# Negations on ScalarE, earlier first tiles, and a new order of a few steps at the joints of a two-layer graph kernel

## The chip, the cores and the metric

The kernel runs on one core of one Trainium2 chip, all in float32. The metric is device time in microseconds (us) of one whole execution. It is read as the median of several runs; a profile is one more execution, with its own time.

## The reference

x is 128 graphs of 64 nodes with 768 features; each graph has a 0/1 adjacency matrix of 64 x 64. After a first layer norm with ReLU, two graph layers follow, and the result is added to x. Cut to what matters:

```python
h = relu(layernorm(x))
for l in range(2):
    m_left  = h @ W_left[l].T ;  m_right = h @ W_right[l].T
    u_left  = h @ m_left^T / sqrt(768) ;  u_right = h @ m_right^T / sqrt(768)   # per graph, 64 x 64
    u = u_left * (upper triangle and diagonal of adj) + u_right * (transposed strict upper triangle)
    e = exp(u) * adj ;  attention = e / (sum(e) + 1e-10)
    h = relu(layer_norm(attention @ (h @ W_lin[l].T + b_lin[l])))
out = x + h
```

## The kernel before, in words

**Units.** The tokens are cut into 16 blocks of 512 (8 graphs each); a block is held transposed, features on the 128 partitions, in one of four tiles `ht0` to `ht3`. Two blocks make a superblock; a layer has eight. The first is called superblock 0 here and the next superblock 1.

**Pass one** of a layer (`pass_one`) computes the left and right products and the scores. A weight matrix is 3 x 3 pieces of 256 x 256, a superblock's tokens are 3 x 4 pieces; instead of 36 products of pieces, the table `PRODUCTS` (numbered 0 to 28) takes 29, of sums of weight pieces (`W_OPS`) with sums of token pieces (`X_OPS`), each once for the left side (k = 0) and once for the right side (k = 1). One such step is 8 matmuls and 8 weight loads on TensorE (PE), L530. The left side sums up in the PSUM banks X, Y and Z, the right side in V, `right0` and `right1`; `read` (L303 on ScalarE for a first value, L221 on VectorE for later ones) takes the banks into the tile `m`. After products 0 and 2 of a superblock the scores of the two blocks of the superblock before follow (`scores`, 192 small matmuls each, L472), and their softmax is a chain of small VectorE, ScalarE and SP steps (`chain`, L476 to L512).

**Superblock 0 of layer one** is special (`first`): it builds the weight sums itself, the left ones on VectorE, most right ones on GpSimd (`weight_op`, L180 to L186, where L186 is a negation: sums 16 and 27 have one each per side). Each finished sum is used by its product and stored to DRAM (`keep_weight`, L194); all later superblocks stream the sums back (`stream`, L197) into a ring of eight tiles `wp0` to `wp7`, each for a left and a right sum. While superblock 0 runs, ring tiles, `ht2`, `ht3` and others serve as single slots for weight sums: `Singles` hands them out by groups, each with the last product up to which a slot may be in use (20, 23, 25 or the end). Streams for products 0 to 4 of superblock 1 are put into SP's queue when product 25 is done (L698 to L700).

**Blocks 2 and 3** are prepared meanwhile: rows of x are loaded (L368), statistics taken on VectorE (L338, L339), scaled on ScalarE (L407, L412), transposed on VectorE (four steps L397 for each block), stored to DRAM in the transposed form (L394, four stores) and loaded back into `ht2` and `ht3` (`load_h`, L373). Blocks 0 and 1 are stored from `ht0` and `ht1` in superblock 1 (L727).

**Pass two** computes h W_lin the same way (15 products, `ORDER`, L1063), multiplies with the attention (L871, L894) and finishes the norm. Where layer two begins, its banks `right0` and `right1` lie where pass two of layer one had its `aux` banks, which are free when the last rows are scaled out of them (L1032, L1034).

**What sets the order.** Nothing is reordered by a scheduler: each engine runs its instructions in the order in which the Python code emits them. PE's steps set the beat: between the halves of a step and after it, `run(slot)` emits what was put into the dictionary `plan` for that slot, or else one item of the list `idle`. A superblock has 116 slots, four for each product. All loads and stores that matter here go through SP's queue, in order; in the built program each also waits until the transfer eight places ahead of it in that queue has landed, apart from its own data.

**Names for the steps of the prediction.** The wait for `SPq L394` is a store of a transposed block; `room<-in_x_dram` (L368) is a load of x rows, here the second half of block 3; `ht<-h` (L373) the load of a transposed block; `wp<-ws` (L197) a stream of a weight tile; `st` (L338) row statistics; `hl` the output of pass two's products; L492 to L506 the softmax (L494 is its exp on ScalarE). At the end of pass one the softmax of the last two blocks is emitted at L790 to L793: the first whole and two steps of the second at once, the rest into slots 3 to 15 of pass two.

Of the kernel before, what the change touches and what calls it, by code (L numbers as in the profile page):

```python
# [10 lines left out]
F32 = mybir.dt.float32  # L11
# [6 lines left out]
def kernel(  # L18
# [12 lines left out]
    nc = tc.nc  # L31
# [43 lines left out]
    def run(slot):  # L75
        if slot in plan:
            for f in plan.pop(slot):
                f()
        elif idle:
            f = idle.popleft()  # L80
            if f is not None:
                f()
# [97 lines left out]
    def weight_op(ss, kind, op, eng):  # L180
        i, o, sign, a, b = op
        t = ss.take((kind, o), LAST_W[o])
        if sign != "neg":
            added(eng, t, sign, ss[kind, a], ss[kind, b])
        else:
            eng.tensor_scalar_mul(t, ss[kind, a], -1.0)  # L186

# [32 lines left out]
    def added(eng, o, sign, a, b):  # L220
        (eng.tensor_add if sign == "+" else eng.tensor_sub)(o, a, b)  # L221
# [26 lines left out]
    def free(key):  # L248
        free_ts.append(held_ts.pop(key))
# [19 lines left out]
    def tokens(l, U, n):  # L269
        if n >= 12:  # L270
            return TS[l, U][n]
        j, k = divmod(n, 4)
        return HT[1, l, 2 * U + k // 2][:, j * K2:(j + 1) * K2, k % 2 * TH:(k % 2 + 1) * TH]
# [110 lines left out]
    def transpose_rows(l, u, pool=None):  # L384

        xr, todo = XR[l, u], []

        def turned(xr, pool):
            xb = blocks_tile(pool)

            def store():
                to = KEPT[l][u].rearrange("(b i) c t -> i c b t", b=4)
                for a in range(4):
                    nc.sync.dma_start(to[:, :, :, a * P:(a + 1) * P],  # L394
                                      xb[a * 32:(a + 1) * 32].rearrange("i (c b) q j -> i c b (q j)", b=4))

            return [lambda q=q: nc.vector.transpose(  # L397
                xb[:, :, q, :], xr[q].rearrange("p (b j) -> p b j", j=32)) for q in range(Q)], store

        if l == 0:  # L400
            mv = stat.tile([P, Q, 2], F32, name="mv0", bufs=2)
            sd = stat.tile([P, Q], F32, name="sd0", bufs=2)
            rs = stat.tile([P, Q], F32, name="rs0", bufs=2)
            nb = stat.tile([P, Q], F32, name="nb0", bufs=2)

            def scale():
                nc.scalar.activation(sd, mv[:, :, 1], AF.Sqrt, bias=eps_in)  # L407
                nc.vector.reciprocal(rs, sd)
                nc.vector.scalar_tensor_tensor(nb, mv[:, :, 0], -1.0, rs, op0=ALU.mult, op1=ALU.mult)

            def norm(q):
                nc.scalar.activation(xr[q], xr[q], AF.Relu, bias=nb[:, q:q + 1], scale=rs[:, q:q + 1])  # L412

            norms = [lambda q=q: norm(q) for q in range(Q)]
            stats = [lambda q=q: mean_var(mv[:, q, :], [xr[q][:, :HH], xr[q][:, HH:]]) for q in range(Q)]
            if u == 3:
                return stats, scale, norms, turned(xr, pool)
            for f in stats + none * (4 * (u < 4)) + [scale] + norms:
                todo.extend([f] + none * (u >= 4))
            todo.extend(none * (2 * (u < 4)))  # L420
        moved, store = turned(xr, pool)
        for f in moved:
            todo.append(f)
            todo.extend(none * (l or u >= 4))
        todo.append(store)
        return todo

# [6 lines left out]
    def pass_one(l, aside):  # L434
        with (tc.tile_pool(name=f"ps_one{l}", bufs=1, space=bass.MemoryType.PSUM) as ps,
# [81 lines left out]

            def project(U, weights, done):
                bank, seen, late = {}, (set(), set()), []
                for i, (w, t, at, new, what) in enumerate(PRODUCTS):  # L520
                    for k in range(2):
                        ns = S - 1 if k and U < NU - 1 else S
                        if new:
                            bank[k, at] = (right[at - 1] if k and at else
                                           ps_st.tile([P, 2 * TH], F32, name="V" if k else "XYZ"[at]))
                        p = bank[k, at][:, :NBB * ns].rearrange("p (g b s) -> p g b s", g=2, s=ns)
                        wk, tk = weights(i, k), tokens(l, U, t)
                        for g in range(2):
                            for c in range(K2):
                                nc.tensor.matmul(p[:, g], wk[:, c, g * P:(g + 1) * P],  # L530
                                                 tk[:, c, :].rearrange("p (b s) -> p b s", s=S)[:, :, :ns],
                                                 start=(new and g == c == 0), stop=(c == K2 - 1),
                                                 skip_group_check=True)
                            if g == 0:
                                run(4 * i + 2 * k)
                        late.append((k, p, ns, what))
                        if k and i in TURNS:
                            if U:
                                scores(2 * U - 2 + TURNS[i], both[TURNS[i]])
                            M[2 * U + TURNS[i]] = sp.tile([P, C, NBB, 2, S], F32, name="m", bufs=2)  # L540
                        now, late = late[::-1], []
                        for kk, pp, n, todo in now:
                            if any(2 * U + int(o, 16) % 4 // 2 not in M for o in todo[1::2]):
                                late.append((kk, pp, n, todo))
                                continue
                            read(pp, lambda o: M[2 * U + o % 4 // 2][:, o // 4 * K2:(o // 4 + 1) * K2,
                                                                     o % 2 * 4:o % 2 * 4 + 4, kk, :n], todo, seen[kk])
                        run(4 * i + 2 * k + 1)
                    for n, last in LAST_X.items():
                        if last == i and n >= 12:  # L550
                            free((l, U, n))
                    done(i)

            def streamed(U):
# [10 lines left out]
            def first():  # L565
# [7 lines left out]
                rest = [spared[:, 2 * n:2 * n + 2].rearrange("p c d -> p (c d)") for n in range(2)]  # L573
                rest.append(big.tile([P, K2, TH], F32, name="ts12", bufs=1).rearrange("p c t -> p (c t)"))
                put(SLOTS - 1, lambda: free_ts.append(12))
                ss = Singles(((20, chunks(2)), (23, chunks(3)), (25, early),
                              (NP, [s.rearrange("p (c d) -> p c d", c=K2) for s in rest]
                               + [room(n, 1).rearrange("p (c d) -> p c d", c=K2) for n in range(12, 15)]
                               + [s for n in range(5, RINGS) for s in pair(NP + n)])))
# [114 lines left out]
                def done(i):  # L694
                    for kind in "lr":
                        keep_weight(0, ss, kind, i)
                        dead(ss, kind, i)
                    if i == 25:  # L698
                        for n in range(5):
                            stream(0, NP + n)  # L700

                return (lambda i, k: ss["lr"[k], PRODUCTS[i][0]]), done

# [16 lines left out]
            for U in range(NU):  # L720
# [3 lines left out]
                    put_token_ops(l, U, "after")  # L724
                if l == 0 and U == 1:
                    for n in range(2):
                        put(20 + 6 * n, lambda n=n: nc.sync.dma_start(KEPT[0][n], HT[1, 0, n]))  # L727
                if U + 1 < NU:
                    def block(n, slot):
                        u = 2 * U + 2 + n  # L730
                        if (l, u) == (0, 3):
                            stats, scale, norms, (moved, store) = transpose_rows(l, u)
                            for fs, at in ((stats[:2], (57, 60)), (stats[2:], (66, 68)), ([scale], (72,)),
                                           (norms, (74, 75, 76, 77)), (moved, (79, 81, 82, 83))):
                                for f, s in zip(fs, at):
                                    put(s, f)
                            put(87, store)
                            put(SLOTS - 4, lambda: load_rows(l, 4))
                            put(101, lambda: load_h(1, l, u))
                            return  # L740
                        *todo, store = transpose_rows(l, u)
                        slot = put_all(slot, todo)
                        put(slot + 6, store)
                        if u + 1 < NB:
                            put(slot + 7, lambda: load_rows(l, u + 1, halves=(1,) if (l, u) == (0, 2) else (0, 1)))
                        slot = max(slot + 15, 92) if U == 0 and l == 0 else slot + 15
                        put(slot, lambda: load_h(1, l, u))
                        if l:
                            put_all(slot + 20, affine(1, l, u))
# [40 lines left out]
            one, two = softmax(NB - 2), softmax(NB - 1)  # L790
            for f in one[:4] + two[:2] + one[4:]:
                f()
            put_all(3, two[2:])  # L793

    rows = {}

# [406 lines left out]
```

## Time and profile before

| | us |
|---|---|
| median of 3 runs | 2714.45 (2713.27 to 2717.49) |
| the profiled execution | 2710.28 |
| its span in the trace | 2708.5 |
| PE busy (matmuls) | 2677.3, 99% of the span |
| VectorE (DVE) busy | 1502.9, 55% |
| GpSimd (POOL) busy | 1380.6, 51% |
| ScalarE (ACT) busy | 829.2, 31% |

The profiled execution took 1.8 us more than its span, and 4.2 us less than the median of the runs; changes in the trace are counted against 2710.28 and then carried over to the median. The span is 99% PE, so the reading is one of gaps: the trace lists, for each group of instructions, the idle time of its engine ahead of it in brackets with what ended it. DVE, ACT and POOL are busy for half the time or less on average; an average over 2.7 ms doesn't tell whether they are full in a stretch of 15 us. A line of the timeline reads: start, duration, engine, line, operation, output<-inputs, sizes, count, and the bracket. SPq is the SP queue issuing a transfer, DMA a transfer on its way. PE's matmul ends are modelled by the profiler, so gaps of a few tenths are rough.

### The profile page before, as it was taken

The numbers are of one execution on the slowest core, as the hardware profiler recorded it, in microseconds if no ns is written. First come the engines' busy times: TensorE is split into PE (matmuls) and PEld (weight loads), VectorE is DVE, ScalarE is ACT, GpSimd is POOL, SyncE is SP. The second block draws the span as 40 slices with busy tenths as digits, with TensorE's granted clock in tenths as the row PEclk, the third lists the DMA queues.
The fourth block names the chain that finished last, engine by engine and source line by source line (L and its number), as shares of the span: only waits on it lengthen the run. The fifth ranks groups of instructions, "written<-read, shape, count | busy, mean of one in ns | idle before, by whom it ended". The sixth has DMA issues, their size and how long they took to land.

```text
span 2708.5 us, 47300 instructions
## 1 busy us (share of the span) xinstructions
PE 2677.3 (99%) x18514; PEld 2304.5 (85%) x18514; DVE 1502.9 (55%) x2458; ACT 829.2 (31%) x1615; POOL 1380.6 (51%) x1071
## 2 busy tenths in 40 slices
PE   9899999999999999999999999999999999999998
PEld 7788888888888888888788888888888888888886
DVE  7665655756647433334343645546446475666667
ACT  4032131321310254454631221221212304445443
POOL 5633244333336776566433325334244286887886
PEclk9999999999999999999999999999999999999999
DMA  8886966858765345558585956958759524655655
GB/s 268 273 304 208 286 204 205 280 203 263 243 209 179 98 144 180 169 168 259 180 279 176 308 190 220 283 185 287 227 194 302 211 79 133 185 157 159 185 156 148
DMA packets 310223, 567.81 MB, mean 210 GB/s; under 512 B 62833, under 2 KB 190065, under 8 KB 301809
## 3 DMA queue, kind: packets, MB, share of 16 engines
q1 hardware_dynamic: 309840, 564.39, 65.1%
q8 instruction: 148, 2.42, 0.4%
q14 instruction: 75, 0.61, 0.1%
q10 hardware_dynamic: 160, 0.39, 0.0%
HBM read 429.40 MB, written 135.27 MB: 208 GB/s over the span
## 4 chain that ended last, share of the span: by engine, by line
PE 94%; DVE 2%; DMA 1%; SPq 1%; issue 0%; ACT 0%; DVEq 0%
PE right L530 17%; PE X L1063 12%; PE X L530 11%; PE V L530 10%; PE Z L530 9%; PE Y L530 9%; PE V L1063 8%; PE Y L1063 6%; PE both L472 5%; PE Z L1063 4%; PE aux L871 2%; PE aux L894 1%; PE Y L894 0%; DMA wp<-ws 0%; PE Z L472 0%
## 5 line engine op out<-in xcount | busy, mean ns | idle before, releaser
L221 POOL TENSOR_TENSOR ts<-ht 128x512 f32<-128x512 f32 x352 | 479.7, 1369 | 160.7 <-PE X L1063 65.9
L221 POOL TENSOR_TENSOR ts<-ht,ts 128x512 f32<-128x512 f32 x192 | 253.0, 1325 | 348.5 <-PE V L530 208.2
L530 PE MATMUL right<-ts,wp 128*128 128x252 f32 (+1 forms) x1632 | 381.1, 377 | 1.5 <-DVE wp L221 1.5
L530 PEld LDWEIGHTS right<-ts,wp 128*128 128x128 f32 x1632 | 310.5, 190 | 40.0 <-DVE wp L221 1.9
L481 POOL TENSOR_TENSOR wm<-adj,tri 128x256 f32<-128x256 f32 x60 | 42.2, 726 | 493.9 <-DMA wp<-ws 220.7
L221 DVE TENSOR_TENSOR m<-m,X 128x512 f32<-128x512 f32 x160 | 105.6, 685 | 259.6 <-ACT m L303 181.3
L221 DVE TENSOR_TENSOR m<-m,right 128x504 f32<-128x504 f32 (+1 forms) x304 | 199.5, 673 | 87.5 <-PE right L530 73.5
L1063 PE MATMUL X<-room,ts 128*128 128x256 f32 x1024 | 244.1, 380 | 0.2
L221 POOL TENSOR_TENSOR ts<-ht,ht 128x512 f32<-128x512 f32 x128 | 163.5, 1288 | 140.0 <-PE right L530 93.7
L530 PE MATMUL Z<-ts,wp 128*128 128x256 f32 x992 | 234.5, 380 | 0.1
L1063 PEld LDWEIGHTS X<-room,ts 128*128 128x128 f32 x1024 | 192.0, 190 | 31.3 <-issue 1.8
L530 PEld LDWEIGHTS Z<-ts,wp 128*128 128x128 f32 x992 | 188.8, 190 | 24.8 <-issue 0.4
L530 PE MATMUL X<-ts,wp 128*128 128x256 f32 x872 | 207.5, 381 | 0.0
L530 PE MATMUL V<-ts,wp 128*128 128x252 f32 (+1 forms) x864 | 201.7, 377 | 0.0
L303 ACT ACTIVATE m<-right 128x504 f32<-128x504 f32 (+1 forms) x64 | 36.1, 590 | 510.2 <-PE both L472 490.3
L380 ACT ACTIVATE ht<-ht,b_col,a_col 128x512 f32<-128x512 f32 x192 | 140.8, 803 | 144.0 <-DMA ht<-h 144.0
L530 PEld LDWEIGHTS X<-ts,wp 128*128 128x128 f32 x872 | 164.9, 190 | 22.8
L1063 PE MATMUL Y<-room,ts 128*128 128x256 f32 x768 | 182.6, 380 | 0.0
L530 PEld LDWEIGHTS V<-ts,wp 128*128 128x128 f32 x864 | 164.4, 190 | 20.2
L1063 PEld LDWEIGHTS Y<-room,ts 128*128 128x128 f32 x768 | 146.1, 190 | 20.1 <-issue 0.6
L221 DVE TENSOR_TENSOR m<-m,Y 128x512 f32<-128x512 f32 x144 | 95.8, 683 | 115.1 <-PE Y L530 104.6
L1029 POOL TENSOR_TENSOR z<-z,b 128x768 f32<-128x768 f32 x62 | 112.6, 1830 | 89.8 <-DVE z L1026 89.8
(225 smaller groups left out, 4845.0 us busy)
## 6 DMA issues: line engine op xcount, KB each, us to landing
wp<-ws SPq DMA_DIRECT2D x435, 512.0 KB, 6.4
ht<-h SPq DMA_DIRECT2D x62, 1536.0 KB, 8.7
h<-room SPq DMA_DIRECT2D x112, 384.0 KB, 6.9
z<-z SPq DMA_DIRECT2D x128, 192.0 KB, 3.1
ws<-wp SPq DMA_DIRECT2D x93, 256.0 KB, 4.4
xr<-in_x_dram SPq DMA_DIRECT2D x120, 192.0 KB, 3.6
out_dram<-xr SPq DMA_DIRECT2D x120, 192.0 KB, 2.6
room<-z SPq DMA_DIRECT2D x112, 192.0 KB, 5.2
```

What stands on the lines that cost most here:

```text
L221: (eng.tensor_add if sign == "+" else eng.tensor_sub)(o, a, b)
L303: nc.scalar.activation(to(o), p, AF.Copy, scale=1.0 if sign == "+" else -1.0)
L380: nc.scalar.activation(ht, ht, AF.Relu, bias=cols[1][:, c:c + 1], scale=cols[0][:, c:c + 1])
L472: nc.tensor.matmul(p[h * S + e:h * S + e + 32, q, e:e + 95], ht[:, c, b * S + e:b * S + e + 32], mb[:, e:e + 95], start=(c == 0), stop=(c ...
L481: nc.gpsimd.tensor_tensor(wm[:, :, k], adj[:, :, 1 - k], tri[:, k].unsqueeze(1).to_broadcast([P, Q, S]), op=ALU.mult)
L530: nc.tensor.matmul(p[:, g], wk[:, c, g * P:(g + 1) * P], tk[:, c, :].rearrange("p (b s) -> p b s", s=S)[:, :, :ns], start=(new and g == c ...
L871: nc.tensor.matmul(cx[k][i, m, :HH], at[j, q, :], hl[j, q, m * HH:(m + 1) * HH], start=True, stop=True)
L894: nc.tensor.matmul(parts[r, k][n][i], at[j, q, :], hl[j, q, cut], start=True, stop=True)
L1029: nc.gpsimd.tensor_add(zs[k], zs[k], rows["b"])
L1063: nc.tensor.matmul(p[:, n], b[t][:, c, r * P:(r + 1) * P], w[s][:, c, :], start=(i in FIRST and i not in PRELOAD and n == c == 0), stop=(c ...
```

## The change

Six edits:

1. A negation of a weight sum that stood on VectorE is done on ScalarE (two instructions, left sums 16 and 27 of superblock 0). Those on GpSimd stay.
2. The four transposing steps of block 2 get an empty slot after each, as those of later blocks have. Its store and the load after it move four slots with them.
3. In superblock 0, the load of transposed block 2 moves from slot 92 to 85, that of block 3 from 101 to 98, the load of the rows of block 4 from slot 112 to 105; the streams of the weight tiles of products 0 and 1 of superblock 1 are put in after product 23 and not 25, for which four single slots are limited to product 23.
4. The stores of blocks 0 and 1 in superblock 1 move from slots 20 and 26 to 26 and 34.
5. In superblock 0 of layer two, the order of the steps is product 0 left, product 1 left, product 0 right, product 1 right and so on; before, product 0 right came second.
6. The last steps of the second softmax at the end of pass one: in place of slots 3, 4, 5, ... they take 6, 9, 12, 13, 14, ...

```diff
-            eng.tensor_scalar_mul(t, ss[kind, a], -1.0)
+        elif eng is nc.vector:
+            nc.scalar.mul(t, ss[kind, a], -1.0)
+        else:
+            eng.tensor_scalar_mul(t, ss[kind, a], -1.0)
...
-            todo.extend(none * (l or u >= 4))
+            todo.extend(none)
...
+                steps = [(i, k) for i in range(NP) for k in range(2)]
+                if l and not U:
+                    steps[1], steps[2] = steps[2], steps[1]
+                for n, (i, k) in enumerate(steps):
...
-                ss = Singles(((20, chunks(2)), (23, chunks(3)), (25, early),
+                ss = Singles(((20, chunks(2)), (23, chunks(3) + early[:4]), (25, early[4:]),
...
-                    if i == 25:
-                        for n in range(5):
-                            stream(0, NP + n)
+                    for n in {23: (0, 1), 25: (2, 3, 4)}.get(i, ()):
+                        stream(0, NP + n)
...
-                        put(20 + 6 * n, lambda n=n: nc.sync.dma_start(KEPT[0][n], HT[1, 0, n]))
+                        put(26 + 8 * n, lambda n=n: nc.sync.dma_start(KEPT[0][n], HT[1, 0, n]))
...
-                            put(SLOTS - 4, lambda: load_rows(l, 4))
-                            put(101, lambda: load_h(1, l, u))
+                            put(SLOTS - 11, lambda: load_rows(l, 4))
+                            put(98, lambda: load_h(1, l, u))
...
-                        slot = max(slot + 15, 92) if U == 0 and l == 0 else slot + 15
+                        slot = max(slot + 15, 85) if U == 0 and l == 0 else slot + 15
...
-            put_all(3, two[2:])
+            put_all(put_all(6, two[2:4], 3), two[4:])
```

The rest of the diff rewrites the loop of `project` over the list `steps`; outside superblock 0 of layer two it emits the same steps in the same order.

## The prediction

> **What bounds the kernel now.** I read the page's first part, then PE's idle times one by one, then SP's and VectorE's timeline ahead of the large ones.
>
> ```profile
> span 2708.5 us, 47300 instructions
> PE 2677.3 (99%) x18514; PEld 2304.5 (85%) x18514; DVE 1502.9 (55%) x2458; ACT 829.2 (31%) x1615; POOL 1380.6 (51%) x1071
> ```
>
> PE is the bound: 31.2 us of the span are not PE, and the change leaves PE's instructions as they are, so 31 us is a ceiling. The timeline of PE gives its stalls (start, duration, ..., in brackets the idle time before and its releaser). The eight that concern the edits:
>
> ```profile
> 57.13 1.97 PE L530 MATMUL Y<-ts,room 128*128 128x256 f32 x8 [0.67 <-DVE room L221]
> 60.55 1.97 PE L530 MATMUL right<-ts,wp 128*128 128x252 f32 x8 [1.46 <-DVE wp L221]
> 88.64 1.97 PE L530 MATMUL Y<-ts,ht 128*128 128x256 f32 x8 [1.82 <-DVE ht L186]
> 122.30 1.97 PE L530 MATMUL Y<-ht,wp 128*128 128x256 f32 x8 [2.58 <-DMA wp<-ws]
> 132.09 1.02 PE L472 MATMUL both<-m,ht 128*32 128x95 f32 x38 [2.75 <-issue]
> ...
> 901.73 1.97 PE L1063 MATMUL X<-room,ht 128*128 128x256 f32 x8 [1.39 <-ACT hl L303]
> ...
> 1363.12 1.94 PE L530 MATMUL right<-ht,wp 128*128 128x252 f32 x8 [1.34 <-DVE z L1032]
> ...
> 2235.92 1.97 PE L1063 MATMUL X<-room,ht 128*128 128x256 f32 x8 [0.67 <-ACT hl L303]
> ```
>
> They sum to 12.7 us. The first five lie in superblock 0 of layer one and the start of superblock 1, the others at three joints. Between them PE is full, so a gain before a stall is kept only if what ends that stall also comes earlier. For that I read SP's timeline:
>
> ```profile
> 61.45 4.66 SPq L394 DMA_DIRECT2D h<-room  x4
> 66.15 1.91 SPq L194 DMA_DIRECT2D ws<-room  x1
> 68.11 1.74 SPq L194 DMA_DIRECT2D ws<-wp  x1
> 69.95 2.26 SPq L368 DMA_DIRECT2D room<-in_x_dram  x4
> ...
> 104.56 0.47 SPq L373 DMA_DIRECT2D ht<-h  x1
> ...
> 112.93 8.73 SPq L197 DMA_DIRECT2D wp<-ws  x5
> ```
>
> and two rows of VectorE's:
>
> ```profile
> 61.30 2.82 DVE L221 TENSOR_TENSOR wp<-ht 128x512 f32<-128x512 f32 x2
> ...
> 87.19 1.30 DVE L186 TENSOR_SCALAR ht<-wp 128x512 f32<-128x512 f32 x1
> ```
>
> The chain of waits follows from the second-half load of block 3 (landed 76.92) through row statistics at 77.15 and a VectorE that is full until the negation ends at 88.49. It also shows the stream at 112.93 released by the block load of 104.56, landing at 112.87: that load stands eight places ahead of it in SP's queue, and SP waits for such a landing.
>
> [...] The nearest row, 128x512 from SBUF to SBUF with bias and scale columns (L380), took 803 ns; I use 0.8[...]. [...] the two sums at 61.30 took 1.41 us each beside a busy GpSimd, a like one at 59.84 0.65. [...] The page's instruction queue q8 shows 148 packets, 2.42 MB, 16.4 KB each; one falls at 98.5 us and the next at 129.5.
>
> **Part by part** (negative is time saved; against the profiled 2710.28).
>
> *Second softmax later (edit 6).* At 901.73 PE waits for the read of bank X by ScalarE, which stands behind the exp at 900.68, and that behind VectorE's sum at 900.23. In the changed order that exp stands behind two more reads. Product 2 ends on PE at 898.45, so the read can be done by 899.25 and PE goes on at 900.34: −1.39; at 2235.92 likewise −0.67. New cover: the rest of VectorE's chain, 4.2 us of steps, now runs from 904.6 to 908.8, and the reads that come next can't start before 909.15 (bank X of product 8): 0.35 us of air at worst. The eight small stores of that softmax stand 7 slots later in SP's queue; their reader is the last block of pass two, hundreds of us later. In layer one six loads of raw weights pass them; nobody waits for those on PE. Sum −2.06.
>
> *Order of two steps (edit 5).* PE's `right` at 1363.12 waits until 1362.98 for the last scaling out of the old banks. Product 1 left (bank Z, free, its weights streamed and its tokens scaled) takes 1.73 us there: `right` could start at 1363.3, after the release: −1.34. `right` ends no later than now, so ScalarE's reads behind it keep their times.
>
> *Negations on ScalarE (edit 1).* The first (36.47 on VectorE, 0.64) gains nothing: the read of Z two instructions later waits for PE's end at 37.46 and started at 37.70. On ScalarE it holds up two copies by some 1.7 us that are used at 46. The second frees VectorE of 1.30 us and shortens PE's wait: 0.8 on ScalarE, 0.5 less. Queued behind it on ScalarE are the four scalings of block 3 (from 85.36); the transposes that need them follow in time.
>
> *Transposes of block 2 spaced (edit 2).* The weight that releases 60.55 loses one transpose (0.89) ahead of it: PE goes on at 59.65. But the next weight sum but two (64.65 to 65.73) stays behind all four transposes, and PE needs it at once: of 0.9 some 0.2 is left at 66.10. What gets later: the last transpose ends at 64.1, not 61.3, so the stores L394 start 2.75 later, and so, past the same two weight stores, does the second-half load of block 3. It lands at 76.92 + 2.75 = 79.7. VectorE stands at its statistics from 77.05: 2.6 us idle. Work from there to the sum that is negated took 77.15 to 87.09; now to 89.7. Plus 0.8: product 20 starts on PE at 90.55 against 88.64, **+1.9**. This contains all gains before it, also 66.10. I take the landing as certain to 0.7 us either way.
>
> *First tiles and block loads sooner (edit 3).* From product 20 to the end of product 28 PE took 88.64 to 119.72, 31.08; so PE reaches superblock 1 at 121.63. Block 2's load is now released by the store of sum 20 (about 94.3) in a stretch where the DMA share was under 0.4, not at 104.56; stream 0 needs the landing of sum 23's store, put at 108 to 110, with no 1.5 MB load right ahead of it, and should land by 115 (9.23 us after its issue, as now, would still be 119). The wait of 2.58 goes, and PE starts at 121.63 instead of 122.30. Net of edits 1 to 3: **−0.67**. Block 3's load lands near 118.5 (now 119.7).
>
> *Then the gap of 2.75 in the scores.* Nothing on the core releases it; a 16 KB instruction packet moves at 129 to 130, PE goes on at 132.09, and the DMA share is 1.01 to 1.07 there. The 31 other scores of the trace have no gap over 0.7. After: 1.57 MB (block 2) has left the full stretch, about 4 us at 400 GB/s, and the eight row loads can start at about 118.6 and not 124.2. The queue is shorter when PE asks, but perhaps not empty. Bounds 0 (or a few tenths worse) and −2.75; I take −2.1, as the queue is nearly through.
>
> *Stores of blocks 0 and 1 (edit 4).* They move 5 to 7 us later; their tiles are reloaded at slot 49, about 12 us after the later start of the first. Streams run eight products, 27 us, ahead. Nothing; without that cover a late stream costs what it lacks.
>
> Sum: −2.06 −1.34 −0.67 −2.1 = −6.2: 2704.1 for a profiled run. The median is 4.2 above the profiled one, so 2708.3.
>
> **Rivals.** (B) *The fetch gap stays.* For it: all bytes but one load are still to be moved before 135. Sum −4.1: 2710.4, and with a half gain 2709.0. (C) *The second-half load isn't late in effect* (DMA is idle from 52 to 62, so two weight stores leave early and the queue is emptier), or VectorE catches up on a quieter GpSimd: product 20 at 88.0 or so, another −1.9 to −2.6: 2705.7 to 2706.4; with the fetch gap as in B, 2707.8. Against it: same four stores, same two stores behind. (D) *Slower: the row load of block 3 is so late that VectorE's wait outweighs all joints.* Product 20 starts 10.85 us after the landing; the total is worse than before when the delay of product 20 is over 2.58 (the wait that it eats) + 3.4 (the joints), a start after 94.6, so from a landing at 83.8, 4.1 later than I put it. At 86 it gives 2714.45 + 8.2 − 2.6 − 3.4 = 2716.7, without any fetch gain. Against it: the chain had 5.15 us from issue to landing under an already full DMA.
>
> **How the numbers follow.** A measurement of this kernel can tell about 0.2%, 5.4 us, from no change: the line is 2709.0. A 0.42 (2707.6 to 2709.0), B 0.33 (2709.0 to 2712), C 0.18 (2704.5 to 2708), D 0.07 (2714.5 to 2718). Faster by over 0.2%: A most of it, C, a little of B: 0.57. Within: 0.39. Slower: D's far end, 0.04. A and C and B up to 2712.5 make the range 2704.5 to 2712.5; it leaves out D and a tail.
>
> **What would show it.** Right: no ScalarE wait at the first X after the joints; `right` at layer two without a wait; statistics of block 3's second half waiting near 79.7 and product 20 waiting longer than 1.82; no wait for wp<-ws at superblock 1. Wrong: a wait on a stream or a block load there, new waits of PE for hl reads after the joints, or a product 20 that starts by 88.6 (then C). The gap in the scores decides A against B.

## The result and the profile after

The changed kernel takes 2706.89 us (median of 14 runs, 2704.2 to 2710.12), the kernel before 2713.13 us in the runs beside them: a ratio of 0.9976, 95% interval 0.9968 to 0.9984. The profiled execution takes 2705.84 us, 4.4 less than that of before. The medians moved by 6.2 (by the interval 4.3 to 8.7).

```profile
span 2704.1 us, 47306 instructions
PE 2677.7 (99%) x18514; PEld 2301.3 (85%) x18514; DVE 1499.1 (55%) x2456; ACT 832.4 (31%) x1617; POOL 1381.4 (51%) x1071
```

PE is busy about as long as before (2677.7 against 2677.3), so what went is idle time. PE's timeline at the places of the prediction:

```profile
59.45 1.97 PE L535 MATMUL right<-ts,wp 128*128 128x252 f32 x8 [0.59 <-DVE wp L223]
80.64 1.94 PE L535 MATMUL right<-ts,ht 128*128 128x252 f32 x8 [0.24 <-DVE m L223]
84.51 1.97 PE L535 MATMUL X<-ts,wp 128*128 128x256 f32 x8 [1.93 <-DVE wp L223]
89.61 1.96 PE L535 MATMUL Y<-ts,ht 128*128 128x256 f32 x8 [1.43 <-ACT ht L186]
120.52 1.89 PE L535 MATMUL Y<-ht,wp 128*128 128x256 f32 x8
130.19 1.02 PE L474 MATMUL both<-m,ht 128*32 128x95 f32 x39 [2.78 <-issue]
...
899.35 1.89 PE L1069 MATMUL X<-room,ht 128*128 128x256 f32 x8
...
1360.90 3.56 PE L535 MATMUL right<-ht,wp 128*128 128x252 f32 x16
...
2231.57 1.89 PE L1069 MATMUL X<-room,ht 128*128 128x256 f32 x8
```

A line without a bracket is work ahead of which the view lists no idle time: the three joints (1.39, 1.34 and 0.67 before) and the start of superblock 1 (2.58 before, now 120.52 instead of 122.30). Three things stay or are new: product 19 left waits 1.93 at 84.51, product 20 starts 0.97 later than before (89.61), and the gap in the scores is 2.78, where it was 2.75.

SP's and VectorE's timelines show why product 20 is later:

```profile
62.60 4.66 SPq L396 DMA_DIRECT2D h<-room  x4
67.30 3.80 SPq L196 DMA_DIRECT2D ws<-wp  x2
71.20 1.94 SPq L370 DMA_DIRECT2D room<-in_x_dram  x4
```

```profile
78.10 1.02 DVE L340 BATCH_NORM_STATS2 st<-room 128x6 f32<-128x384 f32 x2 [2.10 <-DMA room<-in_x_dram]
...
82.74 1.63 DVE L223 TENSOR_TENSOR wp<-ht 128x512 f32<-128x512 f32 x1
```

```profile
88.83 0.63 ACT L186 ACTIVATE ht<-wp 128x512 f32<-128x512 f32 x1 [6.82 <-DVE wp L223]
```

The stores of block 2 start at 62.60 (61.45 before), the load behind them at 71.20 (69.95), and the statistics wait 2.10 for it. From there VectorE is full until the negation on ScalarE, which takes 0.63 us.

Summed at the trace: superblock 1 starts 1.78 earlier, the joints give 3.40, together 5.2; PE's busy time is 0.4 longer and small gaps of a few tenths elsewhere take back about as much. This execution was also 0.3 late from its start (a product that begins at 54.59 in the profile of before begins at 54.89 here), ahead of what the edits change; so of the 0.97 by which product 20 is later, 0.3 are not theirs.

### The profile page after: what moved, and what is told of

Read it like the earlier page. It is cut to its first block, busy times and chain, and to the rows that moved or that the text cites. A ratio compares the mean times of both kernels' runs of the same rounds, so it can differ in the third digit from the quotient of the medians.

```text
span 2704.1 us, 47306 instructions
## 1 busy us (share of the span) xinstructions
PE 2677.7 (99%) x18514; PEld 2301.3 (85%) x18514; DVE 1499.1 (55%) x2456; ACT 832.4 (31%) x1617; POOL 1381.4 (51%) x1071
## 4 chain that ended last, share of the span: by engine, by line
PE 96%; DVE 1%; SPq 0%; issue 0%; DMA 0%; ACT 0%; DVEq 0%; ACTq 0%
PE right L535 17%; PE X L1069 12%; PE X L535 11%; PE V L535 11%; PE Z L535 9%; PE Y L535 9%; PE V L1069 8%; PE Y L1069 6%; PE both L474 5%; PE Z L1069 4%; PE aux L877 2%; PE aux L900 1%; PE Y L900 0%; PE Z L474 0%; DVE wp L223 0%
## 5 line engine op out<-in xcount | busy, mean ns | idle before, releaser
L223 DVE TENSOR_TENSOR hl<-hl,V 128x512 f32<-128x512 f32 (+1 forms) x136 | 89.2, 656 | 128.9 <-PE V L1069 118.7
```

## The experiments

Each ratio is taken against the kernel before in the same session (2712.2 to 2714.0 in the four sessions, which ran on three chips). Where a run is compared with the changed kernel, the difference is that of the two medians, across sessions; through the two ratios it is smaller (2.2 and not 3.4 in experiment 4, 2.4 and not 3.1 in experiment 7). The intervals of experiments 3 to 9, where there is one, all overlap that of the changed kernel, experiment 8's only just. So what a single edit moves is read from the traces. Intervals are of 95%. Undoing an edit means the lines marked with a minus in the diff of the change are put back.

**1. The joints alone** (edits 5 and 6 on the kernel before).

```diff
+                if l and not U:
+                    steps[1], steps[2] = steps[2], steps[1]
...
-            put_all(3, two[2:])
+            put_all(put_all(6, two[2:4], 3), two[4:])
```

> The kernel before with edits 5 and 6 alone (order of two steps at layer two, later steps of the second softmax). Theory: the three waits of 1.39, 1.34 and 0.67 us go and nothing takes their place; superblock 0 of layer one is as before (product 20 waits 1.8, superblock 1 waits 2.6 for its tile): 3.4 us less, about 2709.7 against 2713.1. Rival: PE runs ahead into instruction fetches or reads that come no sooner and gives part back: 1 to 2 us less.

Measured: 2710.16 us, ratio 0.9987 [0.998, 0.9993], 3.5 less (1.9 to 5.4 by the interval). In the trace the three joints have no wait; superblock 0 is as before (product 20 at 88.42 after 1.84, the stream waits 2.92). The prediction's 3.4 for these two edits stands.

**2. Superblock 0 alone** (edits 1 to 4, the joints undone).

```diff
-                if l and not U:
-                    steps[1], steps[2] = steps[2], steps[1]
...
-            put_all(put_all(6, two[2:4], 3), two[4:])
+            put_all(3, two[2:])
```

> The changed kernel with edits 5 and 6 undone: edits 1 to 4 alone. Theory: superblock 1 starts 1.6 us sooner as in the trace of the changed kernel, the gap in the scores stays near 2.8: about 2711.5 against 2713.1. Rival: runs without the profiler often have a smaller gap in the scores, since the median of the changed kernel fell by 6.2 and its traced span by 4.4: then 2.5 to 3.5 us less.

Measured: 2711.11 us, ratio 0.9989 [0.9983, 0.9996], 2.5 less. Product 20 starts at 90.20 after 1.43, superblock 1 at 121.11 without a wait; in the scores there are two gaps, 1.36 and 1.93. With the joints' 3.5 that makes 6.0 of the 6.2: the two halves add up within their intervals. The means differ by 3.1, and the mean granted clock of the runs (0.9982 here, 0.9976 in the runs of before beside them) accounts for 1.8 of it: these runs lost less time at a lower clock, of which experiments 7 to 11 tell more.

**3. Block 2's transposes close together again** (edit 2 undone in the changed kernel).

```diff
-            todo.extend(none)
+            todo.extend(none * (l or u >= 4))
```

> The changed kernel with edit 2 undone (transposes of block 2 close together). Theory: the late second-half load of block 3 is what holds product 20: the load lands near 76 instead of 78.0, product 20 starts at 88.0 to 88.4 instead of 89.6, superblock 1 at about 119.3 instead of 120.7; product 12's right step waits 1.4 again, which is lost in it: 1.4 us less than the changed kernel, 2705.5. Rival: VectorE's work and not its wait sets product 20; it stays at 89.6 or gets later, no gain or 0.5 us more.

Measured: 2705.62 us, ratio 0.9974 [0.9965, 0.9983], 1.3 less than the changed kernel by the medians, with overlapping intervals. Its trace is 2.05 us late from the start for a reason of its own (a wait of 2.08 at 11.56 and a stretch at a clock of 0.50 behind it, 12.09 to 15.50; the product that begins at 54.89 in the changed kernel begins at 56.94). With 2.05 subtracted, product 20 starts at 88.60 (89.61) and superblock 1 at 119.51 (120.52), 1.0 earlier, where 1.2 to 1.6 was expected for product 20. Only 0.3 of it lies ahead of the statistics (77.79 against 78.10, now without a wait); 0.7 lies behind them, where one VectorE sum took 1.18 instead of 1.63, of which the last section tells more. So the trace points to a small cost of edit 2, and neither it nor the medians settle its size.

**4. The load ahead of the stores** (changed kernel; the load of block 3's second half stands before the four stores of block 2 in SP's queue).

```diff
+                        if (l, u) == (0, 2):
+                            put(slot + 6, lambda: load_rows(l, 3, halves=(1,)))
                         put(slot + 6, store)
-                        if u + 1 < NB:
+                        if u + 1 < NB and (l, u) != (0, 2):
```

> The changed kernel with the second-half load of block 3 put ahead of the four stores of block 2 in SP's queue. Theory: it lands near 68, the row statistics wait for nothing, product 19 waits less than 0.3, product 20 starts at 87.4 or sooner, superblock 1 at about 118.5: 2.2 us less than the changed kernel, 2704.7. Rival: VectorE is full of work there, the wait of 2.1 only moves; product 20 gains under 0.5, or the later store delays block 2's load and superblock 1 waits for it.

Measured: 2703.48 us, ratio 0.9968 [0.9955, 0.998], 3.4 less than the changed kernel.

```profile
62.60 1.74 SPq L370 DMA_DIRECT2D room<-in_x_dram  x4
64.39 5.11 SPq L396 DMA_DIRECT2D h<-room  x4
```

```profile
86.72 1.97 PE L535 MATMUL Y<-ts,ht 128*128 128x256 f32 x8 [1.19 <-ACT ht L186]
126.98 1.02 PE L474 MATMUL both<-m,ht 128*32 128x95 f32 x39 [2.46 <-issue]
```

The load leaves SP at 62.60 instead of 71.20, VectorE's statistics start at 75.91 without a wait for it, and product 19's wait is gone. Product 20 starts at 86.72, 2.89 sooner, superblock 1 at 117.63, 2.89 sooner as well. So the late load was the cause of the later product 20. Of the 2.89, 2.19 are the earlier statistics (75.91 against 78.10); the other 0.70 come behind them, mostly from the VectorE sum of 1.63 that took 1.18 here.

**5. The instruction stream shifted** (changed kernel with 64 more PE instructions, 32 tiny matmuls and their weight loads, ahead of product 20). If the gap belongs to a place in PE's instruction stream, it goes or moves; if it belongs to the time, it stays.

```diff
+                    if (l, U, i, k) == (0, 0, 20, 0):
+                        for _ in range(32):
+                            nc.tensor.matmul(both[1][:32, :32], KEEP["ident"][:, :32], KEEP["ident"][:, :32],
+                                             start=True, stop=True)
```

> The changed kernel with 32 tiny matmuls of 32 rows by 32 columns (64 PE instructions with their weight loads) on the unused bank both1 ahead of product 20, in the time in which PE waits there; their result is thrown away. Theory: [...] the gap of 2.8 falls under 0.5, 2.3 us or more less than the changed kernel. Rival: the gap is due to full DMA queues at that time[...], or to the scores' own data: it stays at 1.5 to 3.

Measured: 2705.77 us, ratio 0.9973 [0.9962, 0.9984], 1.1 less than the changed kernel. The first scores, which were cut in two after 153 matmuls, are whole:

```profile
125.81 4.13 PE L474 MATMUL both<-m,ht 128*32 128x95 f32 x192
...
140.49 1.68 PE L474 MATMUL both<-m,ht 128*32 128x95 f32 x72 [0.92 <-issue]
```

The gap of 2.78 is gone, though the transfers on the queues are the same; 0.92 comes back in the second scores, and some tenths elsewhere; every later instruction stands 64 places further on in the stream too. The tiny matmuls take 2.21 us, of which 1.4 lie in the wait that product 20 had anyway. Hence less than expected in time, but the place of the gap follows the instruction. The time at which the scores start is no rival: in experiment 9 the same scores start at 125.75, 0.06 earlier than here, and have a gap of 2.52.

The packet records of the traces show what stands beside these gaps. In the nine kernels that don't shift the stream, a 16 KB packet of the instruction queue q8 begins between 1.2 us before and 0.9 us after PE stops in the first scores, and PE goes on 1.4 to 1.7 us after that packet has ended (in the changed kernel: PE stops at 127.41, the packet runs from 127.56 to 128.58, PE goes on at 130.19). The smaller gaps in the second scores, 0.12 to 1.93 in seven traces, end in the same way, 1.3 to 1.4 after a packet. Here, with the stream shifted, the last packet ahead of the first scores runs at 114.56, eleven us before they start.

**6. Fewer bytes** (changed kernel without six of the eight row loads of block 4, so that block is computed from other rows). If the gap does not depend on the bytes in the queues, it stays.

```diff
-            for a in range(4):
+            for a in range(1 if (l, u) == (0, 4) else 4):
```

> The changed kernel with six of the eight row loads of block 4 left out (1.2 MB less in the stretch ahead of the scores; block 4 is then computed from other rows). Theory of full queues: the fetch comes through sooner, the gap falls under 1.2. [...] the gap stays over 2.

Measured: 2706.82 us in a single run.

```profile
130.16 1.22 PE L474 MATMUL both<-m,ht 128*32 128x95 f32 x39 [3.56 <-issue]
```

Taking 1.2 MB off the queues left the gap, at 3.56, and the packet ahead of its end began later than in any other trace, 0.87 us after PE had stopped. The DMA share at 126 to 132 was still 0.93 to 1.07, so this run does not exclude that empty queues would shorten it; it does show that this much relief doesn't.

**7. Tiles and loads as late as before** (edit 3 undone in the changed kernel).

```diff
...
-                    for n in {23: (0, 1), 25: (2, 3, 4)}.get(i, ()):
-                        stream(0, NP + n)
+                    if i == 25:
+                        for n in range(5):
+                            stream(0, NP + n)
...
-                        slot = max(slot + 15, 85) if U == 0 and l == 0 else slot + 15
+                        slot = max(slot + 15, 92) if U == 0 and l == 0 else slot + 15
```

> The changed kernel with edit 3 undone (loads and first tiles at their old places). Theory: superblock 1 waits for its first tile again, and since the store of block 3 is some 0.5 us later than before, PE starts it at 122.4 to 122.9 instead of 120.7: 1.7 to 2.2 us more than the changed kernel, about 2708.8. Rival: the stalls at products 19 and 20 are what set the start; it stays within 0.5.

Measured: 2710.04 us, ratio 0.9985 [0.9979, 0.9992], 3.1 more than the changed kernel. PE:

```profile
122.60 3.31 PE L535 MATMUL Y<-ht,wp 128*128 128x256 f32 x8 [1.98 <-DMA wp<-ws]
...
134.43 1.81 PE L474 MATMUL both<-m,ht 128*32 128x95 f32 x39 [3.17 <-issue]
```

The wait for the stream is back with 1.98, and superblock 1 starts at 122.60, as expected. But the product behind it took 3.31 us instead of 1.89, and the scores behind the gap 1.81 instead of 1.02. The view by stretches says why (columns: stretch and length, then the busy time of PE, PEld, DVE, ACT and POOL with instruction counts, the granted clock of TensorE, DMA share, GB/s):

```profile
119.70:123.10 3.40, 1.42 (x7) 0.97 (x6) 1.81 (x3) 0.00 (x0) 3.08 (x3) 0.99 1.04 410
123.10:126.50 3.40, 3.40 (x9) 2.70 (x8) 0.00 (x0) 0.00 (x0) 3.32 (x4) 0.50 0.94 290
126.50:129.90 3.40, 3.40 (x107) 2.97 (x109) 0.00 (x0) 0.00 (x0) 3.32 (x3) 1.00 1.00 387
```

After a stretch in which PE was idle for 1.98 us the clock was 0.50 for 3.4 us, and 1.7 us of work were lost on top of the wait. Such stretches come in some executions and not in others: eight of the 21 runs had a mean clock of 0.999 and took 2707.0 us on average, the seven with 0.997 took 2711.3. So part of the 3.1 beyond the expected 1.7 to 2.2 is theirs; how much, the medians don't tell.

**8. Both steps together** (experiments 4 and 5 in one kernel).

> The changed kernel with both: the second-half load of block 3 ahead of the stores of block 2, and the 64 PE instructions ahead of product 20. If the two theories hold and add: 3.0 + 2.3 less than the changed kernel, about 2701.6. If the gap stays, as the kernel with the load first alone, 2703.5.

Measured: 2701.04 us, ratio 0.9956 [0.9944, 0.9969], the fastest kernel here: 5.9 less than the changed one and 12 less than before. It was forecast at 2701.6. Products 19 and 20 do not wait at all, and both scores run whole (`x192`).

**9. The negation back on VectorE** (edit 1 undone in the changed kernel).

```diff
-        elif eng is nc.vector:
-            nc.scalar.mul(t, ss[kind, a], -1.0)
```

> The changed kernel with the four negations of superblock 0 back on VectorE (edit 1 undone), all else kept. Theory: one negation took 0.63 us on ScalarE in the changed kernel and 1.4 us or so beside VectorE's full stretch before; of block 3's chain to product 20 one negation lies on the path, so product 20 starts 0.6 to 1.0 us later (about 90.4 instead of 89.61) and superblock 1 at about 121.4 instead of 120.68, with the gap in the scores of 2.3 to 3.2 us as it is: 2707.5 to 2708 (+0.7 to +1.0). Rival, in which the negations don't lie on the path since the load of block 3's rows sets the end: superblock 1 at 120.7, 2706.9 (no change from the changed kernel).

Measured: 2707.66 us, ratio 0.9978 [0.997, 0.9986]: 0.8 more than the changed kernel, too little for the intervals to tell. Product 20 did not start near 90.4, as expected, but at 89.63. Still the trace shows the edit: product 20 started 11.13 us after the statistics of block 3's second half (78.50 to 89.63), where experiments 6 and 7, with the negation on ScalarE, took 10.43 and 10.45: 0.7 for the edit. (The superblock start that this expectation calls 120.68 reads 120.52 in the trace, and edit 1 moves two negations, not four.) In the changed kernel and experiment 2 the same way took 11.5 and 11.6, since one sum of VectorE (82.74) took 1.63 and 1.77 instead of 0.68. That difference of 1.0 is not this edit's: it goes with how the sum meets one of GpSimd (last section).

```profile
83.96 1.97 PE L533 MATMUL X<-ts,wp 128*128 128x256 f32 x8 [0.98 <-DVE wp L221]
89.63 3.65 PE L533 MATMUL Y<-ts,ht 128*128 128x256 f32 x8 [2.00 <-DVE ht L186]
```

Here too the product behind the wait of 2.00 took 3.65. Such a slow product follows some waits of about 2 us and more and not others (the product behind the 2.58 of before took 1.97). The next two runs ask when.

**10 and 11. Stalls of a chosen length** (experiment 8's kernel with 14 stalls in layer one; N is 1, then 4).

```diff
+                    if U and l == 0 and (i, k) in ((20, 0), (26, 0)):
+                        nc.tensor.matmul(both[1][:32, :32], KEEP["ident"][:, :32], KEEP["ident"][:, :32],
+                                         start=True, stop=True)
+                        nc.scalar.copy(KEEP["probe"][0][:32, :32], both[1][:32, :32])
+                        for a in range(N):
+                            nc.scalar.mul(KEEP["probe"][1 - a % 2], KEEP["probe"][a % 2], 1.0)
+                        nc.tensor.matmul(both[1][:32, :32], KEEP["probe"][N % 2][:, :32], KEEP["probe"][N % 2][:, :32],
+                                         start=True, stop=True)
```

> The fastest version so far (e8_best) with 14 stalls put into layer one: in superblocks 1 to 7, ahead of products 20 left and 26 left, a tiny matmul, a short read of its bank by ScalarE, one ScalarE operation of 128x384 and a tiny matmul that reads it. Each should hold PE for 1.1 to 1.5 us. Theory (a stall of 2.0 us or more inside one stretch of 3.41 us of TensorE's clock grid is followed by a stretch of 3.41 us at half clock, 1.7 us more; a shorter one costs only itself): no half-clock stretch, PE busy as in e8_best (2680.0) within 1 us, time 2701.0 plus the sum of the stalls, 15 to 21 us: 2716 to 2722. Rival (any stall of over 1 us can be followed by half clock, at random): several half-clock stretches among the 14, PE busy 5 us or more higher.

> As the run with short stalls, but with four ScalarE operations of 128x384 in each of the 14 stalls, so that each holds PE for 2.5 to 3.1 us. Theory: of a stall of 2.8 us, 1.97 us or more fall within one stretch of the 3.41 us grid in 0.66 of the phases ((3.41 - 2.8) + 2 x (2.8 - 1.97), over 3.41), so about 9 of 14 are followed by half clock, each 1.7 us: PE busy about 16 us higher than in e8_best, 2695, and the time 2701.0 + 39 + 16 = 2756. Rival (the length of a stall doesn't bring the half clock, the stalls seen before were chance): PE busy as in e8_best within 4 us, time about 2740.

Measured: 2742.6 us (ratio 1.0108 [1.0091, 1.0125]) and 2780.52 us (1.0246 [1.0231, 1.0261]). Both times missed, by 20 us and more, for one reason that I had not foreseen: ahead of product 20, in six of seven superblocks, the first tiny matmul itself waited for the softmax mask that still read its bank (1.65 us, once 4.40 or 3.40), so that two stalls stood 0.25 us apart there. The short run's 8 clean stalls were of 0.87 us, and none was followed by half clock; its five stretches at half clock all lie behind the double ones, against the expectation of none (PE busy 15.0 more than in experiment 8, where at most 1 was expected). In the long run 8 stalls were clean, all of 2.54 us, and four were followed by half clock:

```profile
342.50:345.00 2.50, 0.03 (x2) 0.00 (x0) 1.16 (x2) 2.25 (x5) 0.00 (x0) 1.00 1.07 317
345.00:348.40 3.40, 3.33 (x9) 2.71 (x10) 0.00 (x0) 0.02 (x1) 2.86 (x4) 0.50 0.63 259
223.70:226.25 2.55, 0.02 (x1) 0.00 (x0) 1.15 (x2) 2.26 (x5) 0.59 (x1) 1.00 1.01 346
226.25:229.70 3.45, 3.45 (x17) 3.06 (x18) 0.69 (x1) 0.00 (x0) 3.37 (x5) 1.00 0.38 153
```

Two equal stalls, two outcomes: 9 matmuls in 3.40 us at 0.50, or 17 in 3.45 us at full clock. The changes of clock in one execution lie whole multiples of 3.413 us apart (in experiment 7 it falls at 123.06 and 133.30, three of them, and in experiment 3 at 12.09 and 131.56, 35 of them), so I laid this grid over the eight stalls, and took the larger part of each that falls in one stretch:

| stall starts | larger part in one stretch, us | clock of the next stretch |
|---|---|---|
| 821.87 | 1.56 | 1.00 |
| 462.76 | 1.69 | 1.00 |
| 223.71 | 1.81 | 1.00 |
| 938.19 | 1.82 | 1.00 |
| 701.28 | 2.11 | 0.50 |
| 912.89 | 2.12 | 0.50 |
| 581.58 | 2.34 | 0.50 |
| 342.53 | 2.46 | 0.50 |

The order is clean, and the other traces bring the border closer. The waits of 1.98 and 2.00 in experiments 7 and 9 lie whole in one stretch and were followed by half clock. The 1.93 at product 19 of the changed kernel lies whole in one stretch too, and of the 2.08 there in experiment 5 the larger part is 1.97: neither was followed. The 2.58 of before is cut by the grid into 1.89 and less, and its 2.75 into 1.44 and less, so its profile has no such stretch. The rival of chance fails: for a stall in one piece, 1.97 us of idle PE in one stretch was the most that passed, and 1.98 the least that did not.

Stalls in pieces are another matter. In the short run two stretches with 1.64 and 1.71 us of idle PE, cut into two by tiny matmuls, were followed by half clock; in the long run one with 1.82, cut in the same way, was not. And a stretch already at half clock needed less: with 0.70 us and more of idle PE it was followed by another (seven cases), with 0.42 and less it was not. As an estimate, both borders leave about the same work done in the stretch: 3.41 − 1.97 is 1.44 us at full clock, and half of 3.41 less 0.42 to 0.70 is 1.36 to 1.50. The sum of the long run closes as well: against experiment 8 the long run's stalls add 46.9 us (8 x 2.54 + 6 x 2.48 + 5 x 1.65 + 3.40) and its PE busy time 27.6, 74.5 together, and its span is 73.4 longer.

## Why the prediction was right, point by point

*Joints (edits 5 and 6), −3.40:* right in mechanism and size; measured −3.5 alone. The cover held: VectorE's later softmax steps ended at 906.8, ahead of its next read at 908.25; forecast was 0.35 us of air, it was 1.4.

*Transposes spaced (edit 2), product 20 at 90.55:* right in kind, too large: 89.61. Of the two terms that were off, the first is the end of the last transpose, put at 64.1: it was 62.5, since the two sums that now stand ahead of it took 0.68 and 0.87 us and not 1.41 each as before, so the stores started 1.15 later and not 2.75, and the statistics at 78.10 and not 79.7. The second is the negation, 0.63 us and not the 0.8 that I took from the row with bias and scale columns (803 ns). Against both stood a sum of 1.63 us on the way, which took 1.18 before. The late load and this sum together made the wait of 1.93 at product 19 (0.98 with the sum at 0.68 in experiment 9, none in experiment 4, where the load was early), which no step of mine named. So one of the signs failed: product 20 waited 1.43 and not longer than 1.82, since part of the wait had moved ahead of it. Experiment 4 puts the late load at 2.2 us.

*Earlier tiles (edit 3):* right. The wait of 2.58 went, the first streams landed 3.2 to 4.1 us after their issue from 109.30 on (9.23 before). In both traces each of 1773 transfers left SP's queue after the landing of the eighth ahead of it, the closest by 0.02 us. Net of edits 1 to 3: forecast −0.67, measured −1.78. The row loads of block 4 were issued at 123.38; I had put them at 118.6, and experiment 6, with six of the eight left out, has the gap all the same.

*The gap in the scores, −2.1:* this step failed: +0.03. I argued that less queued DMA would let the instruction packet in sooner (at an estimated 400 GB/s; the trace of before has 421 at 114 to 118 and 388 at 118 to 122). The gap stands behind the same instruction, 153 or 154 matmuls into the scores, in every kernel that doesn't shift the stream (2.33 to 3.56; 1.36 in experiment 2, with another 1.93 later), with 1.2 MB less as with all, and goes when 64 instructions are put ahead. A 16 KB packet of instructions ends in each of these gaps or shortly ahead of it (experiment 5), so the packet was the right thing to look at; what I had wrong is that fewer bytes would bring it sooner. Queue q8 moves 148 such packets for 37,028 matmuls and weight loads, 250 to a packet on average. 192 small matmuls with their weight loads are 384 instructions in some 4 us (4.13 in experiment 8), more than one such share. That the place in the stream decides is shown (2.78 in the changed kernel, no gap there in experiment 5). That PE stands there because it waits for the packet is my estimate, from the 1.4 to 1.7 us between the packet's end and PE's going on; when the packet is asked for, and how soon it would come on empty queues, isn't shown, since no run had them empty there.

*Edit 4, nothing:* nothing in the trace contradicts it; it wasn't tried alone.

So by mechanism it is case B (−4.1 forecast; the trace has −4.4). The median, 2706.89, lies below the bands given for A and for B and in the one given for C, though product 20 did not start where C wants it: the kernel before took 2713.13 us in the runs beside it, and not the 2714.45 of three runs from which the bands were counted. And that the medians moved by the 6.2 of the forecast is luck: the gap gave nothing of its 2.1, superblock 0 gave 1.1 more than forecast, small gaps and busy time took back 0.8, and the medians moved 1.8 more than the traces.

One cause for those 1.8 follows from experiments 7 to 11, and the record can test it, since it has the mean granted clock of each run. In the 100 runs of before beside the experiments, the ten with 0.999 took 2710.8 us on average, the fifty with 0.998 2712.6, the 35 with 0.997 2715.3: over all 100, 0.98 us of time go with each us of clock lost (the share not granted, times the span), so most of the spread between runs goes with the clock. The profiled execution of before (0.999, no stretch at half clock until its end) is near the short end of these. If the phase is taken as random, with a border of 1.97 us, the stalls of 2.58 and 2.75 would be followed by half clock in 0.60 and 0.65 of executions (for the first, (3.41 − 2.58) + 2 x (2.58 − 1.97), over 3.41); at 1.7 us each that is an estimate of 2.1 us that before carries. Measured by the mean clock, it loses 2.6 us more than experiment 8, which has no such stall (0.9976 and 0.9986). But the changed kernel, for whose one stall of 2.78 the same estimate is 1.1, loses 2.2 more than experiment 8 (0.9978). So the clock accounts for 0.4 us, with a standard error of 0.6, of the difference. The rest of the 1.8 stays open; it is inside the interval of the medians.

## What to carry to other kernels

Here a stall of an otherwise full TensorE with 1.98 us or more in one stretch of 3.413 us cost 1.7 us more than it shows, so stalls of 2 to 3 us are the first to shorten, even by half. Breaking one up was not enough where the pieces stood close: the short run had pieces of 1.65 and 0.82 us 0.25 us apart, and at three of five such places (424.71, 539.17, 653.34) half clock followed. Before spreading work over more slots, follow each queue entry that moves with it: here four stores went 1.15 us later, and statistics waited 2.10 us for the load that stood behind them; put ahead of them it kept nobody waiting. Here a gap that nothing on the core released, in a stretch of dense small instructions, ended 1.3 to 1.7 us after a 16 KB packet of the instruction queue, and 64 instructions put ahead of it moved it: look for such a packet, and let a shift tell. And when timed runs of one kernel spread, set them beside their granted clock before looking elsewhere (here 0.98 us of time went with each us of clock lost).

## What was not expected of the hardware

The half clock stood in no step of the prediction. In one execution the clock changes whole multiples of 3.413 us apart, and from one execution to another the grid is shifted: the fall at 89.72 in experiment 9 is 33.34 us from the one at 123.06 in experiment 7, which is 9.77 steps. PE need not be idle for a whole stretch: for a stall in one piece, 1.98 us of idle time in a stretch were enough, 1.97 were not. The lower clock, 0.50, then held for one stretch (or two, as in experiment 7 from 133.30, where PE was idle for another 1.13 us in the first).

VectorE's plain 128x512 sum (82.74 in the changed kernel) took from 0.68 to 1.78 us at the same place in the programs, enough to move product 20 by 1.0 us. GpSimd's sums beside it show what goes with it; first the changed kernel, then experiment 6:

```profile
82.56 1.26 POOL L223 TENSOR_TENSOR ts<-ts,ht 128x512 f32<-128x512 f32 x1
```

```profile
82.99 0.68 DVE L223 TENSOR_TENSOR wp<-ht 128x512 f32<-128x512 f32 x1
82.99 1.82 POOL L223 TENSOR_TENSOR ts<-ts,ht 128x512 f32<-128x512 f32 x1
```

In the changed kernel GpSimd's sum had begun 0.18 us earlier, and VectorE's ended 0.55 us after it. In experiment 6 both began in the same hundredth; VectorE's ran in 0.68, and GpSimd's took 1.82. In ten of the thirteen traces GpSimd's sum has begun first, and VectorE's ends 0.55 us after it; in three (experiments 6, 7 and 9) VectorE's comes first and takes 0.68 to 0.71. In all thirteen the next sum of GpSimd ends 1.13 to 1.14 us after VectorE's. So at this place one of the two came first and the other ended behind it, VectorE's 0.55 us, GpSimd's 1.13 to 1.14, and the 1.0 us at product 20 goes with which of them came first. Why the second takes longer, and what settled the order in experiment 6, the traces don't show.
